# Moving the conditioning of batches 1 to 3 behind a transpose, and reordering a list of steps, in a gated quantised layer on one core

## The chip, the cores and the metric

The kernel runs on one core of a Trainium2 chip. A core has five engines with an instruction queue each: TensorE (PE, matmuls and transposes), VectorE (DVE), ScalarE (ACT), GpSimd (POOL) and SyncE (SP), which here only issues DMA transfers. Each queue is worked off strictly in its order, and the engines wait for one another on semaphores. The metric is the device time of one execution in microseconds (us), the median of several executions; lower is better.

## The reference

For `x` of 4 batches x 1024 tokens x 512, `cond` of 4 x 128, `norm_w` of 512 x 128, `up_w` of 4096 x 512 and `down_w` of 512 x 2048:

```python
scale = cond @ norm_w.T + 1.0                      # (batch, 512): the conditioning
ms = mean(x * x, axis=-1)
h = x * (scale[:, None, :] * rsqrt(ms + 1e-6))
val, gate = split(h @ up_w.T, 2)                   # 2048 each
h = val * gelu(gate)
hq = act_quant(h)                                  # 8 bit, one scale a token
wq = weight_quant(down_w)                          # -1, 0, 1 with one scale
y = hq @ wq.T + x
```

## The kernel before, in words

**Tiling.** The up projection is worked off in 16 slots a batch; a slot takes 128 columns of the gate and the 128 of the value that belong to them, against all 1024 tokens in two halves of 512. Operands are split in a high and a low float16 part, so that a product has twelve matmuls of 128x512 (two by four high-low terms and four high-high). In the first batch slots 0 to 13 are such plain products (`gate.j.h`, `value.j.h` for slot `j` and half `h`); later slots use a scheme with fewer products (`slot.g.n`), which needs sums of blocks of weights and of x that the first batch prepares. The down projection of a batch runs inside the slots of the next.

**Order of the work.** The order on every engine is written out by hand: instructions are issued in the order of the Python statements. Three pieces follow one another: the *head* (statements at the end of the function, from `first_load(0, 2)` on), `plain_first` (slot 0 for the first half of the tokens, with `second_part` and `second_slot` put between its matmuls), and `take(FIRST_BATCH)`, a string of 599 steps for slots 1 to 15 of the first batch. A step `name.a.b` calls an entry of the table `STEPS`; a name given to two engines has a last figure, 1 for VectorE and none for GpSimd. A step issues to whichever engines it needs, also to SyncE's queue.

**The head.** Loads go to SyncE: `norm_w`, x in four parts (`first_load`, two tiles of 128 tokens each), and the first weights (`w_load(0)` to `w_load(2)`). Meanwhile:

- `keep_warm(n)` runs `n` matmuls on zeros (`pz`, 128x512), whose result nobody reads.
- `cond_first_row` spreads `cond[0]` over the partitions by a matmul (`pc`), `cond_scale(0, pc)` multiplies and sums it with `norm_w` on VectorE, `cond_largest` takes the largest magnitude (`mx`), `cond_over` transposes that on TensorE (`pm`), `cond_range_steps` makes a power of two of it on VectorE, and `cond_spread` brings it to all partitions by a matmul (`pd`): the conditioning of batch 0.
- `cond_turn` transposes `cond` (`pc_t`) and `norm_w` in four blocks (`nw_t`) on TensorE and copies both out on ScalarE (`cT`, `nwT`). `cond_scale_rest` multiplies them in four small matmuls of float32 (`ps`, three columns each) and ScalarE adds 1 and writes `scT[:, :, 1:]`: the conditioning of batches 1 to 3. Its first reader is the step `c_largest` of the list.
- `first_sum` takes the sum of squares of a tile of x, `rsqrt_root` and `rsqrt_steps` its inverse root, `first_scale` scales the tile, `first_turn` transposes it on TensorE into the banks `ptx`, and `first_high` and `first_low` write its high and low parts with the conditioning (`XP`).
- `w_largest`, `w_factor_steps`, `w_scale`, `w_turn` (bank `pw`), `w_high` and `w_low` do the like with the weights of slot 0.

**The list.** `turn.n`, `x_scale.n`, `x_high.k` and `x_low.k` are the same for tiles 4 to 7. `w_load.j`, `w_range.j`, `w_factor.j` and `w_scale.j.t` load and scale the weights of slot `j`; `rows_high`, `rows_low` and `rows_turn` split them and transpose them by DMA; `s_sum.j.n`, `s_high.j.n`, `s_low.j.n` and `s_spill.j.n` make the sums of blocks and store them. `d_load.n` loads a part of `down_w` and `d_sum.n` sums its magnitudes on ScalarE; parts 2 and 3 go where `first_sum` writes its unread squares (`junk`). `o_*` and `t_*` prepare sums of x, `max.*` collects the largest magnitudes a token, `c_*` ends the conditioning of batches 1 to 3.

The lines of the profile that matter here: L1172 `keep_warm`, L207 `pc`, L185 and L189 `cond_turn`, L186 and L190 its copies, L197 and L202 `cond_scale_rest`, L228 `pm`, L253 `pd`, L1122 `first_sum` on ScalarE, L1149 `first_scale` on ScalarE, L1156 `first_turn`, L378 `w_turn`, L411 `w_high`, L1160 `first_high`, L779 the products of slot 0, L708 the plain products after it, L318 `w_range` on ScalarE, L302 `w_load` from 3 on, L305 the earlier ones, L511 `d_load`.

Of the kernel before, what the change touches and what calls it, by code (L numbers as in the profile page):

```python
# [14 lines left out]
AF = mybir.ActivationFunctionType  # L15
# [36 lines left out]
def glu_quant_kernel(  # L52
# [17 lines left out]
    NK = D // P  # L70
# [93 lines left out]
    def bank(tag, bufs, shape=None, name=None):  # L164
        return psum.tile(shape or [P, TOK], F32, name=name or tag, tag=tag, bufs=bufs)
# [26 lines left out]
    def cond_scale_rest():  # L192

        n = B - 1
        ps = bank("E", 2, name="ps")[:, : NK * n]
        for k in range(NK):
            PE.matmul(  # L197
                ps[:, k * n : (k + 1) * n], nwT[:, k * P : (k + 1) * P], cT[:, 1:B],
                start=True, stop=True,
            )  # L200
        v = ps.rearrange("p (k b) -> p k b", b=n)
        ACT.activation(scT[:, :, 1:], v, AF.Copy, bias=1.0)  # L202
# [145 lines left out]
    def w_range(j, t0=0, t1=2):  # L348
        w_factor(j, w_largest(j, t0, t1), t0, t1)
# [818 lines left out]
    def keep_warm(n):  # L1168

        pz = bank("A", 2, name="pz")  # L1170
        for i in range(n):
            PE.matmul(pz, warm[:, :P], warm, start=True, stop=True)  # L1172
# [10 lines left out]
    cond_turn()  # L1183
# [7 lines left out]
    cond_scale_rest()  # L1191
    keep_warm(4)
    steps = cond_range_steps(pm, 0, 1)
# [5 lines left out]
    keep_warm(7)  # L1199
# [69 lines left out]
    def next_turn(n):  # L1269
        if not made:  # L1270
# [75 lines left out]
    def take(steps):  # L1346
# [11 lines left out]
        o_WHOLE.3.2.1 w_range.4 d_load.0 rows_low.3 value.1.1 gelu.1.1 s_high.0.1 t_square.0.0 s_low.0.1.1  # L1358
        s_spill.0.0 s_sum.1.3.1 s_high.1.0 w_factor.4 w_load.10 w_range.5 out.0.1 rows_turn.3 gate.2.0
        s_low.1.0.1 s_high.1.1 w_scale.4.1 w_factor.5 s_low.1.1 out.1.1 d_sum.5 value.2.0 s_sum.2.1  # L1360
        w_scale.5.0 s_sum.2.0.1 w_scale.5.1 o_sum.0 d_sum.6 s_sum.2.2 c_over w_scale.4.0 gate.2.1 d_load.1
        c_range s_sum.2.3 s_spill.1.0 rows_high.4 s_spill.2.1 d_sum.7 w_gain.2 o_sum.1 gelu.2.0 value.2.1
        rows_low.4 o_high.1 out.2.0 w_gain.4 rows_high.5 o_low.1 w_load.6 gate.3.0 gelu.2.1 o_sum.2
        s_high.2.0 rows_turn.4 s_high.2.1 o_sum.3 o_high.2 value.3.0 o_high.3 rows_low.5 s_spill.3.1
        gelu.3.0 rows_turn.5 o_low.2 d_sum.2 gate.3.1 out.2.1 t_square.0.1 max.0.0.0 d_sum.3 t_root.0
        d_sum.0 s_low.2.0.1 s_spill.2.0 value.3.1 o_low.3 w_range.6 s_sum.3.0 w_load.7 d_sum.1 s_spill.4.1
        w_factor.6 s_low.2.1 w_load.11 w_scale.6.0 c_spread s_sum.3.1.1 s_spill.2.2 c_rows gate.4.0 out.3.0
        o_high.0 w_scale.6.1 o_low.0 gelu.3.1 rows_high.6 out.3.1 value.4.0 s_sum.3.2.1 w_range.7 max.1.0.0
        s_sum.3.3 w_load.8 s_high.3.1 rows_low.6 rows_turn.6 gelu.4.0 gate.4.1 s_high.3.0 s_low.3.0
        s_low.3.1.1 c_copy w_factor.7 w_scale.7.1 max.0.1.0 w_scale.7.0 t_load.1 value.4.1 out.4.0 s_sum.4.0  # L1370
        rows_high.7 rows_low.7 rows_turn.7 gelu.4.1 w_range.8 gate.5.0 s_sum.4.1.1 d_total s_sum.4.2.1
        out.4.1 s_high.4.0 s_sum.4.3.1 w_factor.8 s_spill.5.1 s_low.4.0 c_undo w_scale.8.1 c_store value.5.0
        s_sum.5.1.1 s_spill.3.2 w_scale.8.0 s_spill.6.1 w_gain.6 c_load gelu.5.0 s_sum.5.0.1 rows_high.8
        max.1.0.1 d_spread out.5.0 gate.5.1 w_range.9 rows_low.8 s_spill.7.1 s_high.4.1 s_low.4.1 max.1.1.0
        value.5.1 rows_turn.8 s_sum.5.2.1 s_high.5.0 s_sum.5.3.1 c_bring gelu.5.1 max.1.1.1 s_high.5.1
        s_low.5.0.1 gate.6.0 w_factor.9 s_sum.6.1 d_mean w_scale.9.0 t_scale.0.1 w_scale.9.1 out.5.1
        s_spill.5.0 t_high.0.1 s_spill.3.0 t_scale.0.0 value.6.0 gelu.6.0 s_spill.8.1 max.2.0.0 t_sum.0.1
        rows_high.9 s_low.5.1 t_high.0.0 s_sum.6.0.1 s_sum.6.2.1 s_high.6.0 gate.6.1 t_low.0.0 s_sum.6.3
        t_sum.0.0.1 rows_low.9 value.6.1 rows_turn.9 gelu.6.1 max.2.0.1 w_gain.8 t_sum.0.2.1 w_range.10
        t_sum.0.3 t_high.0.2 w_factor.10 gate.7.0 s_low.6.0.1 w_scale.10.1 out.6.0 w_scale.10.0 t_low.0.2  # L1380
        rows_high.10 s_spill.4.0 s_spill.5.2 value.7.0 t_low.0.1 t_turn.0 s_sum.7.1.1 out.6.1 rows_low.10
        w_range.11 gate.7.1 s_sum.7.0.1 s_sum.7.2 s_high.6.1 s_low.6.1.1 t_square.1.0 max.2.1.0 t_square.1.1
        s_sum.7.3 s_high.7.0 s_spill.4.2 t_root.1 value.7.1 s_spill.9.1 gelu.7.0 max.2.1.1 s_spill.6.0
        s_high.7.1 s_low.7.1 rows_turn.10 w_factor.11 s_low.7.0.1 gate.8.0 s_sum.8.0.1 s_sum.8.2.1 out.7.0
        gelu.8.0 max.3.0.0 s_spill.7.0 s_spill.6.2 value.8.0 s_sum.8.1.1 s_sum.8.3.1 w_gain.10 t_scale.1.1
        gelu.7.1 s_high.8.0 s_low.8.0.1 s_spill.8.0 s_high.8.1 gate.8.1 w_scale.11.1 w_scale.11.0
        s_sum.9.0.1 out.7.1 s_low.8.1.1 s_sum.9.2.1 value.8.1 s_sum.9.1.1 s_high.9.0 s_sum.9.3.1 w_load.12
        t_sum.1.0.1 s_low.9.0.1 rows_high.11 s_spill.8.2 w_range.12 rows_low.11 rows_turn.11 gate.9.0
        max.3.0.1 out.8.0 t_scale.1.0 value.9.0 s_spill.9.0 t_sum.1.1 gelu.8.1 t_load.2 gelu.9.0 w_factor.12
        s_spill.11.1 out.8.1 w_scale.12.1 s_sum.10.0.1 w_scale.12.0 t_sum.1.2.1 gate.9.1 s_high.9.1  # L1390
        s_sum.10.1.1 rows_high.12 t_sum.1.3 max.3.1.0 s_spill.7.2 s_low.9.1 t_high.1.2 s_sum.10.2.1
        max.3.1.1 t_high.1.1 value.9.1 s_high.10.0 s_sum.10.3.1 w_load.13 rows_low.12 t_high.1.0
        rows_turn.12 t_low.1.1 s_high.10.1 t_low.1.2 gelu.9.1 gate.10.0 w_range.13 t_low.1.0 out.9.0
        s_low.10.0.1 t_turn.1 value.10.0 max.4.0.0 s_sum.11.0 gelu.10.0 s_low.10.1 out.9.1 s_sum.11.2.1
        s_sum.11.1.1 s_high.11.0 max.4.0.1 gate.10.1 s_sum.11.3.1 t_square.2.1 s_low.11.0.1 s_sum.12.0
        s_spill.12.1 s_high.11.1 w_factor.13 w_load.14 s_spill.11.0 s_low.11.1.1 value.10.1 gelu.10.1
        s_sum.12.2.1 s_spill.10.1 t_load.3 t_square.2.0 w_scale.13.0 t_root.2 w_scale.13.1 s_sum.12.1
        gate.11.0 t_scale.2.1 out.10.0 t_high.2.1 s_spill.9.2 rows_high.13 t_scale.2.0 rows_low.13
        rows_turn.13 s_high.12.0 value.11.0 w_range.14 s_low.12.0.1 s_sum.13.1 t_high.2.0 out.10.1 gate.11.1
        w_factor.14 s_sum.12.3 w_scale.14.1 s_spill.10.2 t_low.2.1 s_sum.13.0.1 s_spill.10.0 w_scale.14.0  # L1400
        t_sum.2.1.1 s_spill.11.2 t_sum.2.0.1 w_gain.12 value.11.1 s_spill.12.0 s_sum.13.2.1 gelu.11.0
        t_sum.2.2 t_sum.2.3.1 w_load.15 gelu.11.1 s_high.12.1 out.11.0 s_high.13.0 s_low.13.0 s_spill.13.0
        out.11.1 gate.12.0 t_low.2.0 t_high.2.2 value.12.0 gelu.12.0 t_low.2.2 w_range.15 t_turn.2
        s_low.12.1 max.4.1.0 t_square.3.0 s_sum.14.1 gate.12.1 t_square.3.1 s_sum.13.3.1 w_factor.15
        rows_high.14 t_root.3 s_sum.14.0.1 max.4.1.1 s_sum.14.2 rows_low.14 value.12.1 gelu.12.1
        rows_turn.14 w_scale.15.1 w_scale.15.0 out.12.0 out.12.1 rows_high.15 gate.13.0 s_high.13.1
# [403 lines left out]
```

## Time and profile before

| | |
|---|---|
| median of 3 timed runs | 725.05 us (725.01, 725.05, 727.67) |
| the profiled execution's own time | 727.31 us |
| its span, first to last instruction | 725.4 us |
| TensorE busy | 718.4 us, 99% |
| VectorE, ScalarE, GpSimd busy | 584.5, 419.9, 139.1 us |
| DMA | 122.64 MB, mean 169 GB/s |

Of the views, the page gives busy times and shares; the waits say who stood still, for whom, in total, how often and the longest; the chain of waits follows the work that ended last back from the end; timelines give the start, the duration, engine, line and operation, output and inputs of instructions, and in brackets how long the engine stood idle before and what ended it. A matmul's duration includes its way through the array, so that consecutive matmuls overlap: the time that one costs is the distance between two starts.

### The profile page before, as it was taken

To read this page: it belongs to the slowest core of one execution; us is meant where nothing else is said; L and a number is where in the kernel's file an instruction comes from. 1 tells how busy PE (TensorE), PEld (TensorE's weight loads), DVE (VectorE), ACT (ScalarE), POOL (GpSimd) and SP (SyncE) were. 2 spreads that over 40 slices of the span, in tenths; PEclk is the share of its full clock that TensorE was granted. 3 is DMA by queue.
4 is the path that set the end of the run, shared out by engine and by line. 5 is a ranking of instruction groups with operands and counts; after the bars stand their busy time and mean duration, and the time that the engine had idled before them with its cause. 6 is when DMAs were issued, how large, how long until landed. Compare 5 with 4: busy or idle time off the path is not lost.

```text
span 725.4 us, 10231 instructions
## 1 busy us (share of the span) xinstructions
PE 718.4 (99%) x3679; PEld 362.7 (50%) x3679; DVE 584.5 (81%) x876; ACT 419.9 (58%) x697; POOL 139.1 (19%) x143
## 2 busy tenths in 40 slices
PE   8999999999999999999999999999999999999998
PEld 5444444444444446665444445666444444445854
DVE  6789799875898899788689887777678888765896
ACT  5899767774766775544335676544433665333463
POOL 1722231352100033540000030360020000000120
PEclk9999999999999999999999999999999999999999
DMA  7799978999995655877845647765955455453253
GB/s 275 261 246 275 249 184 242 277 204 259 290 200 122 131 122 152 198 182 153 189 101 103 131 101 175 203 148 155 218 97 112 103 102 102 102 100 99 102 166 126
DMA packets 228405, 122.64 MB, mean 169 GB/s; under 512 B 189801, under 2 KB 199805, under 8 KB 228354
## 3 DMA queue, kind: packets, MB, share of 16 engines
q1 hardware_dynamic: 228202, 121.85, 68.2%
q8 instruction: 29, 0.48, 0.3%
q14 instruction: 22, 0.18, 0.1%
q10 hardware_dynamic: 152, 0.13, 0.1%
HBM read 53.50 MB, written 23.09 MB: 106 GB/s over the span
## 4 chain that ended last, share of the span: by engine, by line
PE 93%; DVE 4%; ACT 1%; DMA 1%; issue 0%; SPq 0%
PE A L693 33%; PE E L693 17%; PE pv L708 9%; PE po L1055 9%; PE pg L708 9%; PE B L693 9%; PE po_end L1007 4%; DVE gm L899 1%; PE pz L1172 1%; DMA H<-in_L_cond_up_w_dram 1%; DVE R L901 1%; DVE R L894 1%; ACT R L1160 1%; DVE H L828 0%; DVE t L836 0%
## 5 line engine op out<-in xcount | busy, mean ns | idle before, releaser
L693 PEld LDWEIGHTS <-SXY 128*128 128x128 f16 x2058 | 201.4, 98 | 236.0 <-issue 0.7
L693 PE MATMUL A<-R,SXY 128*128 128x512 f16 x1158 | 267.4, 379 | 0.0
L693 PE MATMUL E<-R,SXY 128*128 128x512 f16 x582 | 141.4, 379 | 0.1
L828 DVE SCALAR_TENSOR_TENSOR H<-A,sg,t 128x512 f32<-128x512 f32 x50 | 37.5, 749 | 72.0 <-PE A L693 71.8
L979 DVE TENSOR_TENSOR H<-H,am 128x1024 f32<-128x1024 f32 x64 | 76.1, 1214 | 0.0
L839 ACT ACTIVATE t<-t,sg 128x512 f32<-128x512 f32 x50 | 36.1, 721 | 65.9 <-DVE t L836 65.8
L693 PE MATMUL B<-R,SXY 128*128 128x512 f16 x294 | 71.5, 379 | 0.0
L899 DVE TENSOR_REDUCE gm<-H 128x512 f32<-128x1024 f32 x56 | 69.0, 1233 | 0.9
L708 PEld LDWEIGHTS <-SXY 128*128 128x128 f16 x438 | 42.8, 98 | 53.3 <-issue 1.9
L915 POOL PARTITION_ALL_REDUCE am<-R x8 | 14.4, 1795 | 229.3 <-DVE R L901 229.3
L822 ACT ACTIVATE t<-B,sg 128x512 f32<-128x512 f32 x50 | 34.4, 687 | 38.8 <-PE B L693 38.2
L708 PE MATMUL pg<-R,SXY 128*128 128x512 f16 x228 | 52.7, 379 | 1.3 <-ACT R L1160 1.3
L1055 PE MATMUL po<-wd,R 128*128 128x256 fp8e4 x416 | 52.4, 273 | 0.0
L708 PE MATMUL pv<-R,SXY 128*128 128x512 f16 x210 | 48.9, 379 | 0.0
L815 ACT COPY t<-A 128x512 f32<-128x512 f32 x50 | 29.0, 581 | 34.3 <-PE A L693 33.9
L1055 PEld LDWEIGHTS <-R 128*128 128x128 bf16 (+1 forms) x448 | 43.8, 98 | 8.9
L808 ACT COPY v<-E 128x512 f32<-128x512 f32 x50 | 29.3, 586 | 32.0 <-PE E L693 28.4
L800 ACT COPY B<-A 128x512 f32<-128x512 f32 x50 | 28.6, 572 | 31.7 <-PE A L693 31.1
L848 DVE SCALAR_TENSOR_TENSOR H<-v,sg,t 128x512 f32<-128x512 f32 x50 | 39.3, 786 | 7.2 <-ACT t L839 7.2
L845 DVE TENSOR_TENSOR v<-A,v 128x512 f32<-128x512 f32 x50 | 34.1, 683 | 13.1 <-PE A L693 11.9
L987 ACT ACTIVATE H<-H 128x1024 f32<-128x1024 f32 x38 | 39.9, 1050 | 5.2 <-DVE H L979 5.2
L901 DVE TENSOR_TENSOR R<-R,gm 128x512 f32<-128x512 f32 x56 | 40.7, 727 | 1.0
(237 smaller groups left out, 935.3 us busy)
## 6 DMA issues: line engine op xcount, KB each, us to landing
SXY<-s_dram SPq DMA_DIRECT2D x48, 256.0 KB, 3.0
H<-in_L_cond_up_w_dram SPq DMA_DIRECT2D x13, 512.0 KB, 5.5
s_dram<-SXY SPq DMA_DIRECT2D x17, 384.0 KB, 3.4
SXY<-s_dram SPq DMA_DIRECT2D x48, 128.0 KB, 3.4
xr<-in_x_dram SPq DMA_DIRECT2D x19, 256.0 KB, 3.2
out_dram<-xr SPq DMA_DIRECT2D x19, 256.0 KB, 3.0
H<-in_x_dram SPq DMA_DIRECT2D x8, 512.0 KB, 5.3
R<-in_L_cond_down_w_dram SPq DMA_DIRECT2D x8, 512.0 KB, 7.4
```

Of the source, the lines that this page charges most:

```text
L693: PE.matmul(o, s[:, w, k, :], operand(g // NJ, c, l, k), start=start and n == 0, stop=stop and n == len(TERMS) - 1, skip_group_check=True,)
L708: PE.matmul(ps, a[k // 2][:, w, k % 2, :], XP[:, l, k, h * TOK : (h + 1) * TOK], start=n == 0, stop=n == len(terms) - 1,)
L822: ACT.activation(self.t1, self.B, AF.Gelu, scale=gain(self.g, 1))
L828: DVE.scalar_tensor_tensor(h_half(self.g, 0), self.A, gain(self.g, 0), self.t1, ALU.mult, ALU.mult)
L839: ACT.activation(self.t2, self.t2, AF.Gelu, scale=gain(self.g, 1))
L845: DVE.tensor_tensor(self.v, self.A, self.v, ALU.add)
L848: DVE.scalar_tensor_tensor(h_half(self.g, 1), self.v, gain(self.g, 0), self.t2, ALU.mult, ALU.mult)
L899: DVE.tensor_reduce(gm[0], v, AX.X, ALU.max, apply_absolute_value=True)
L901: return [largest, lambda: DVE.tensor_tensor(m, m, gm[0], ALU.max)]
L979: DVE.tensor_tensor(v, v, r.to_broadcast([P, 2, TOK]), ALU.mult)
L987: ACT.activation(v, v, AF.Copy, bias=MAGIC)
L1055: PE.matmul(po, w[:, j], m, start=start and j == 0, stop=stop and j == n - 1, skip_group_check=True,)
```

## The change

In the head, `cond_turn` moves from ahead of the second group of idle matmuls to behind the fourth call, that is behind `cond_over` (the transpose of the maximum). The matmuls of `cond_scale_rest` are taken apart: those for blocks 0 and 1 go between idle matmuls behind `cond_spread`, where instead of seven idle matmuls there are two groups of two; those for blocks 2 and 3 go behind the transpose of slot 0's gate weights, and the ScalarE operation that ends them behind `w_high(0, (1,))`. There are 16 idle matmuls for 19. A test in `next_turn` is written differently and does the same.

```diff
-    def cond_scale_rest():
+    def cond_scale_rest(ps, ks):
         n = B - 1
-        ps = bank("E", 2, name="ps")[:, : NK * n]
-        for k in range(NK):
+        for k in ks:
             PE.matmul(
                 ps[:, k * n : (k + 1) * n], nwT[:, k * P : (k + 1) * P], cT[:, 1:B],
                 start=True, stop=True,
             )
-        v = ps.rearrange("p (k b) -> p k b", b=n)
-        ACT.activation(scT[:, :, 1:], v, AF.Copy, bias=1.0)
...
-    def keep_warm(n):
-        pz = bank("A", 2, name="pz")
+    def keep_warm(n, pz=None):
+        pz = pz or bank("A", 2, name="pz")
...
     pc = cond_first_row()
-    cond_turn()
     keep_warm(5)
     cond_scale(0, pc)
...
     root = rsqrt_root(0, 2)
-    cond_scale_rest()
     keep_warm(4)
+    cond_turn()
     steps = cond_range_steps(pm, 0, 1)
...
     pd = cond_spread(dg, 0, 1, "A")
-    keep_warm(7)
+    ps = bank("E", 2, name="ps")[:, : NK * (B - 1)]
+    pz = bank("A", 2, name="pz")
+    for k in range(2):
+        cond_scale_rest(ps, (k,))
+        keep_warm(2, pz)
     first_sum(2)
...
     w_turn(0, [bank("E", 2, name=f"pw_0_{t}") for t in (1, 0)], (1,))
+    cond_scale_rest(ps, (2, 3))
     w_range(0, 0, 1)
     first_high(0, 0, ptx[0])
     w_high(0, (1,))
+    ACT.activation(
+        scT[:, :, 1:], ps.rearrange("p (k b) -> p k b", b=B - 1), AF.Copy, bias=1.0
+    )
     w_scale(0, (0,))
```

The list has the same 599 steps in another order. Most steps move by a few places. Eight change their engine: `s_sum.0.3`, `s_sum.1.0`, `s_sum.14.2` and `s_sum.15.2` go from GpSimd to VectorE, `s_sum.1.3`, `s_sum.8.1`, `s_low.8.1` and `s_low.15.0` from VectorE to GpSimd. Its beginning, up to the second slot:

```diff
-        d_load.6 d_load.5 d_load.3 w_load.3 d_load.4 t_load.0 d_load.7 s_sum.0.0 o_whole.2.2.0 gate.1.0
-        x_scale.6 w_range.3 x_scale.7 s_sum.0.1 gelu.1.0 turn.4 turn.5 w_load.4 w_factor.3 s_sum.0.2 turn.6
-        w_range.2 turn.7 o_whole.0.0.0 w_load.5 x_high.0 value.1.0 x_high.3 x_low.0 d_load.2 x_high.1
-        s_high.0.0 w_factor.2 s_sum.0.3 w_load.9 x_high.2 s_low.0.0 x_low.1 w_scale.2.1 x_low.2 w_scale.2.0
-        x_low.3 gate.0.1 o_whole.1.0.1 w_scale.3.1 out.1.0 rows_high.2 value.0.1 gelu.0.1 rows_low.2
-        rows_turn.2 d_sum.4 s_sum.1.0 w_scale.3.0 gate.1.1 s_sum.1.1.1 rows_high.3 s_sum.1.2 c_largest
+        d_load.7 w_load.3 d_load.3 d_load.5 d_load.4 t_load.0 d_load.6 s_sum.0.0 o_whole.2.2.0 gate.1.0
+        x_scale.6 w_range.3 x_scale.7 s_sum.0.2 turn.4 w_range.2 turn.5 w_load.4 s_sum.0.1 turn.6 w_factor.3
+        turn.7 o_whole.0.0.0 d_load.2 x_high.0 value.1.0 w_load.5 gelu.1.0 x_low.0 x_high.1 x_high.2
+        w_factor.2 x_low.1 x_high.3 w_scale.2.1 x_low.3 o_whole.1.0.1 s_high.0.0 x_low.2 gate.0.1
+        w_scale.2.0 out.1.0 w_scale.3.1 s_low.0.0 value.0.1 rows_high.2 w_scale.3.0 rows_low.2 rows_turn.2
+        rows_high.3 s_sum.1.0.1 gate.1.1 w_range.4 o_WHOLE.3.2.1 s_sum.1.1.1 d_sum.4 s_sum.0.3.1 d_load.0
+        rows_low.3 w_load.9 gelu.1.1 value.1.1 s_sum.1.2 c_largest t_square.0.0 gelu.0.1 s_high.0.1
```

More of the change, by code (lines that the diff above doesn't have):

```diff
@@ L1357, in glu_quant_kernel @@
-        rows_turn.2 d_sum.4 s_sum.1.0 w_scale.3.0 gate.1.1 s_sum.1.1.1 rows_high.3 s_sum.1.2 c_largest
[L1358 to L1371, printed above, removed]
@@ L1387, in glu_quant_kernel @@
[L1387 to L1396, printed above, removed]
@@ L1402, in glu_quant_kernel @@
[L1402 to L1406, printed above, removed]
@@ new lines, in glu_quant_kernel @@
+        rows_turn.3 w_scale.4.1 w_factor.5 s_high.1.1 out.1.1 value.2.0 d_sum.5 s_low.1.1 w_scale.5.1
+        s_low.1.0.1 d_sum.6 s_sum.2.1 w_scale.4.0 c_over s_sum.2.0.1 s_sum.2.2 gate.2.1 o_sum.0 w_gain.4
+        d_sum.7 c_range s_spill.1.0 rows_high.4 s_sum.2.3 d_load.1 s_spill.2.1 value.2.1 w_scale.5.0
+        w_gain.2 o_sum.1 gelu.2.0 out.2.0 o_high.1 rows_low.4 rows_turn.4 gelu.2.1 gate.3.0 rows_high.5
+        o_low.1 s_high.2.0 o_sum.2 s_high.2.1 value.3.0 o_sum.3 o_high.2 w_load.6 o_high.3 rows_low.5
@@ new lines, in glu_quant_kernel @@
+        rows_turn.5 gelu.3.0 gate.3.1 out.2.1 d_sum.2 o_low.3 d_sum.3 max.0.0.0 s_spill.3.1 t_square.0.1
+        value.3.1 d_sum.0 o_low.2 w_range.6 t_root.0 s_low.2.0.1 s_spill.2.0 c_spread d_sum.1 c_rows
+        gate.4.0 w_load.7 w_factor.6 s_sum.3.0 s_spill.4.1 w_scale.6.0 out.3.0 w_load.11 o_high.0 s_low.2.1
+        s_spill.2.2 s_sum.3.1.1 w_scale.6.1 o_low.0 value.4.0 gelu.3.1 rows_high.6 out.3.1 s_sum.3.2.1
+        s_sum.3.3 w_range.7 max.1.0.0 gate.4.1 w_load.8 s_high.3.1 rows_low.6 rows_turn.6 gelu.4.0
@@ new lines, in glu_quant_kernel @@
+        s_spill.10.1 s_sum.11.2.1 s_sum.11.1.1 s_high.11.0 gate.10.1 max.4.0.1 s_sum.11.3.1 t_square.2.1
+        s_low.11.0.1 s_sum.12.0 s_spill.12.1 s_high.11.1 w_load.14 gelu.10.1 w_factor.13 s_spill.11.0
+        s_low.11.1.1 value.10.1 s_spill.9.2 s_sum.12.2.1 t_load.3 t_square.2.0 w_scale.13.0 t_root.2
+        t_scale.2.1 w_scale.13.1 s_sum.12.1 gate.11.0 t_high.2.1 out.10.0 rows_high.13 t_scale.2.0
+        rows_low.13 rows_turn.13 s_high.12.0 value.11.0 w_range.14 s_low.12.0.1 s_sum.13.1 t_high.2.0
```

79 lines of the change are left out of this document (46 added, 33 removed).

## The prediction

> **What bounds the kernel now.** I read the page first, then TensorE's waits, then the chain of waits in order of time, then the timelines of the first 34 us by engine. The page:
>
> ```profile
> span 725.4 us, 10231 instructions
> PE 718.4 (99%) x3679; PEld 362.7 (50%) x3679; DVE 584.5 (81%) x876; ACT 419.9 (58%) x697; POOL 139.1 (19%) x143
> PEclk9999999999999999999999999999999999999999
> ```
>
> TensorE (PE) is busy in all but 7 us. Everything it waits for in the whole span stands in one view, its waits (total us, times, longest):
>
> ```profile
> PE pz L1172 <- DVE eps L1102: 1.5, 1, 1.5
> PE pg L708 <- ACT R L1160: 1.3, 2, 0.9
> PE pg L779 <- ACT SXY L411: 0.7, 1, 0.7
> PE pg L779 <- ACT R L1160: 0.2, 1, 0.2
> ```
>
> So a change of order can gain in two places: these waits, all in the first 33 us, and time in which PE is busy with idle matmuls (`pz`) or runs slowly. After that PE never waits for another engine, and a reordering there can only lose. The chain of waits through the head (start, us, what):
>
> ```profile
> 3.72 0.01 PE pc_t L185
> 3.73 1.04 PE nw_t L189 x4
> 4.77 2.13 PE pz L1172 x5
> 6.91 0.21 PE pm L228
> 7.12 1.50 PE ps L197 x8
> 8.62 1.73 PE pz L1172 x4
> 10.35 0.51 PE pd L253 x2
> 10.86 2.46 PE pz L1172 x7
> 13.32 1.75 PE ptx L1156 x16
> 15.07 0.45 PE pw L378 x4
> ```
>
> Two readings. First, idle matmuls stand directly ahead of the transposes of x (`ptx`), though x was ready: ScalarE ends its three scalings at 11.61 (9.68 + 1.93, below), and `ptx` begins at 13.32. PE's own queue sets the head. Second, PE doubles its pace on the way: a 128x128 transpose takes 0.26 us in `nw_t` (1.04/4) and 0.11 in `ptx` (1.75/16); `pz` goes from 0.43 (1.73/4) to about 0.22. The granted clock on the page reads full throughout, so only the spacing shows it. Three looks at PE's timeline, each row beginning at the first matmul then running:
>
> ```profile
> 12.05 0.85 PE L1172 MATMUL pz<-H 128*128 128x512 f16 x2
> 12.47 0.85 PE L1172 MATMUL pz<-H 128*128 128x512 f16 x3
> 12.73 0.59 PE L1172 MATMUL pz<-H 128*128 128x512 f16 x2
> ```
>
> Starts at 12.05, 12.47, 12.73: the pace doubles near 12.5, some 4 us into the idle matmuls that began at 8.62 (only `pd` between). The nine earlier ones were split by `nw_t` and `ps` and did not do it.
>
> **The head, part by part.** The timelines of ScalarE (ACT) and VectorE (DVE), and the first product on PE:
>
> ```profile
> 4.81 0.59 ACT L190 COPY R<-nw_t 128x512 f32<-128x512 f32 x1 [0.85 <-PE nw_t L189]
> 8.66 0.18 ACT L202 ACTIVATE scT<-ps 128x12 f32<-128x12 f32 x1 [1.65 <-PE ps L197]
> 8.73 0.62 ACT L1122 ACTIVATE R<-H 128x512 f32<-128x512 f32 x1
> 9.68 1.93 ACT L1149 ACTIVATE H<-H,rs 128x512 f32<-128x512 f32 x3
> 5.29 0.16 DVE L221 TENSOR_REDUCE mx<-scT 128x1 f32<-128x4 f32 x1
> 7.16 0.28 DVE L236 TENSOR_REDUCE d<-pm 1x1 f32<-1x128 f32 x1 [0.55 <-PE pm L228]
> 16.19 0.39 PE L779 MATMUL pg<-R,SXY 128*128 128x512 f16 x1 [0.68 <-ACT SXY L411]
> ```
>
> *`cond_turn` moved behind `pm`.* 1.05 us of PE (0.01 + 1.04) leaves the place ahead of the five `pz`; they now end at 5.85, and `pm` runs to 6.06 since `mx` is ready at 5.45. DVE loses its wait of 0.55. The four `pz` end at 7.79 and `pc_t`, `nw_t` at 8.84 at the slow pace. What is new: ACT's copy of `nwT` (0.59) ends at 9.46, and behind it in ACT's queue stands the sum of squares that ran at 8.73, so ACT's chain slips by 0.73 and its scalings end at 12.34. `pd` (0.51) fits beside the copy.
>
> *`cond_scale_rest` split, `pz` 19 to 16.* PE now waits for the copy (9.46), then two steps of 0.38 (a quarter of 1.50) and four `pz` of 0.43: 0.76 + 1.73, so `ptx` begins at 11.96, 1.36 us earlier. The first scaling is there at 9.68 + 0.73 + 0.64 = 11.05. The two later steps lie behind `pw` in PE's wait of 0.7 for ACT and cost nothing; uncovered they would be 0.75. ACT's `scT` (0.18, of which 0.07 shows: 8.66 to 8.73) now stands ahead of three casts that PE needs: +0.1. Its reader, `c_largest`, stands in the list behind `gate.1.1`, far from it.
>
> What that gives depends on when the pace doubles, which no trace shows for the new order. Bounds from the rows:
> - as late as now (12.5): 0.54 us of `ptx` at 0.21, then 13.5 at 0.11 = 1.47, `pw` 0.45: end 14.42 for 15.52. Head -1.1 + 0.1 = -1.0.
> - inside the nine `pz` that now stand almost together from 3.72 to 7.79 (4.07 us with 0.21 of `pm`, as long as the stretch that did it before): `pc_t` and `nw_t` take 0.5, the copy ends at 8.92, ACT slips by 0.19 only; `ptx` is then paced by the scalings, the last at 11.80, and ends at 12.24 for 15.07: -2.8 + 0.1 = -2.7.
>
> I take -2.4: the nine stand as dense as the run that worked, and 0.3 is kept back because `pw` still waits for GpSimd's scaling of the weights and the loads arrive when they did.
>
> The Trainium skill, "TensorE: Matmul & The Clock Gate", Part 1, says the same of the mechanism: the array runs at half rate until one free-running window of about 3.4 us has been busy. The trace agrees: the pace doubled after 3.9 us of unbroken idle matmuls. Taken strictly the rule speaks against the value above, since 4.07 us contain a whole window of 3.4 only in one phase of five (0.67 of 3.4), and the head would then give -1.0 in the others; by the row, where `pd` did not spoil the stretch, it gives -2.4.
>
> **The list.** The same 599 steps. SyncE's queue in the head, what it waited for, the median time of such a load to landing, and the stretch on ACT and PE that follows:
>
> ```profile
> 8.26 12.45 SPq L511 DMA_DIRECT2D R<-in_L_cond_down_w_dram  x3
> 20.76 0.43 SPq L302 DMA_DIRECT2D H<-in_L_cond_up_w_dram  x1
> SPq L511 <- ACT R L1122: 10.2, 1, 10.2
> R<-in_L_cond_down_w_dram SPq DMA_DIRECT2D x7, 512.0 KB, 7.7
> 27.34 0.63 ACT L318 ACTIVATE H<-H 128x512 f16<-128x512 f32 x1 [2.64 <-DMA H<-in_L_cond_up_w_dram]
> 26.82 1.04 PE L1156 MATMUL ptx<-ident,H 128*128 128x128 f32 x8
> 30.29 0.38 PE L708 MATMUL pg<-R,SXY 128*128 128x512 f16 x1
> 31.04 0.38 PE L708 MATMUL pg<-R,SXY 128*128 128x512 f16 x1 [0.37 <-ACT R L1160]
> 32.35 1.89 PE L708 MATMUL pg<-R,SXY 128*128 128x512 f16 x8 [0.94 <-ACT R L1160]
> ```
>
> Of the three issues from 8.26 the third, `d_load.3`, writes where the sums of squares put their junk, and waits 10.2 us for the last. `w_load.3` stood behind it, issued at 20.76; ACT waited 2.64 for it at 27.34, with four casts of x behind that, and PE lost 0.37 + 0.94 = 1.31. Now `w_load.3` is second, ahead of `d_load.3`. It takes the place of a load of the same size issued within a microsecond of 8.26, so it is there near 17 (7.7 from issue to landing), against a need at 24.7 (27.34 less 2.64). ACT's wait of 2.64 goes; next late for the casts is PE's own transpose of x (26.82 + 1.04 = 27.9), and four casts with one GELU, at about the scalings' 0.64, end at 31.1, when PE asks for the last one (30.29 + three of 0.22 = 30.95). I take -1.3; the ends are -1.31 and 0. `d_load.6`, `d_load.5` go the other way, into the burst that `d_load.3` opens near 20; they are first read by `d_sum`, behind `gate.1.1`. `d_load.2` passes `w_load.5`, which lands one load of 512 KB later for it; its reader `w_range.5` stands several products behind.
>
> Behind that the list has reorderings within a slot and eight changes of engine, four each way, between GpSimd and VectorE:
>
> ```profile
> L432 DVE TENSOR_TENSOR H<-H x37: 405/417/949, 36.5 to 158.9; 128x256 f32<-128x256 f32 x37
> L432 POOL TENSOR_TENSOR H<-H x27: 723/730/3647, 22.5 to 165.3; 128x256 f32<-128x256 f32 x27
> 33.00:60.00 27.00, 27.00 (x127) 12.29 (x126) 24.06 (x37) 26.63 (x50) 9.56 (x10) 1.00 0.92 257
> 90.00:120.00 30.00, 30.00 (x141) 13.59 (x139) 28.39 (x50) 20.26 (x41) 7.24 (x10) 1.00 0.80 211
> ```
>
> (The last two: stretch, then busy time of PE, PEld, DVE, ACT, POOL.) At 0.42 against 0.73 us each the exchange evens out, and neither engine is ever waited for by PE. ACT from 33 to 60 (26.63 of 27) and DVE from 90 to 120 (28.39 of 30) are the covers that could fail. The first comes in 2.64 us better off. Bounds 0 and +1.3, the wait that PE knew here when a load was late; I take 0.
>
> **Sum.** Against the profiled execution's own 727.31 us: -2.4 - 1.3 + 0 = 723.6; with the bounds -4.0 to +0.3. That execution lies 2.26 above the median of the timed runs (725.05) and near their highest (727.67). I read the lower runs as ones without the late load or with an earlier doubling, that is with part of the gain already in them, and so keep 723.7 and not 725.05 - 3.7.
>
> **Rivals.**
> - *The doubling comes too late (slower).* The idle matmuls behind `nw_t` come in twos now, between small steps and a wait; if the nine do not do it, nothing dense follows until the products. `ptx` and `pw` then take 20 x 0.21 = 4.2 from 11.96, the first product follows 0.68 later, near 16.9 for 16.19 (+0.8 with `scT`), and every further us at the slow pace costs half. With 1.3 won at the load it decides from 18.0 on; at 22.7 it is +0.8 + 2.85 - 1.3 = +2.3: 729.6. For it: the earlier nine `pz` failed when split. Against: unsplit, they are as long as the run that worked. The same page of the Trainium skill (Part 4) holds that transposes do not count as activity, which this trace allows (`nw_t`, slow, brought nothing) and which speaks for this rival.
> - *Doubling where it was.* -1.0 - 1.3: 725.0.
> - *The gain adds to the median.* If the 2.26 are the profile's own cost, 725.05 - 3.7 = 721.4. Against it: a timed run reached 727.67 without one.
> - *A new wait in the list.* One cast or turn late in slots 1 to 3 takes the 1.3 back: 725 to 726.5. PE's waits show no margin to judge it by, only that there was none.
>
> **How the numbers follow.** Forecast 723.7 with 0.45, the later doubling 0.17, the gain on the median 0.13, too late 0.15, a new wait 0.10. A measurement here tells about 0.5% (3.6 us) from no change: under 721.4 is half of the third case and some of the first, 0.14; over 728.7 is most of the too-late case and a little of the last, 0.14; between, 0.72. The range 721.0 to 728.3 takes in all but the ends of both; the likeliest case alone has 722.5 to 725.
>
> **What would show it.** Right: `ptx` begins at 10.5 to 12, L776 (the old L779) before 15.3, `w_load.3` issued near 9, no wait of PE on ACT near 31, and none later. The spacing of the second group of `pz` tells the clock: 0.43 to the end, with transposes of 0.21, is the too-late case. A wait of PE between 33 and 180 us is the new wait. Wrong altogether: spans of PE's work that differ after 180 us, where nothing was edited.

## The result, and the profile after

The changed kernel takes 723.91 us (median of 20 timed executions, 722.68 to 726.55), the kernel before 725.37 (20 executions in turn with them, 724.56 to 729.50): a ratio of 0.9973, 95% interval 0.9961 to 0.9985. The profiled execution of the changed kernel took 724.24 us with a span of 722.5, against 727.31 and 725.4 before.

First the page of the changed kernel (span; busy time of the engines) and the waits of PE (for whom; us in total, times, longest):

```profile
span 722.5 us, 10223 instructions
PE 716.2 (99%) x3676; PEld 360.7 (50%) x3676; DVE 584.4 (81%) x876; ACT 420.0 (58%) x697; POOL 139.4 (19%) x143
```

```profile
PE pz L1169 <- DVE eps L1099: 1.5, 1, 1.5
PE ps L196 <- ACT R L190: 0.4, 1, 0.4
PE pg L776 <- ACT SXY L408: 0.3, 1, 0.3
PE pg L776 <- ACT R L1157: 0.3, 1, 0.3
PE A L690 <- DMA SXY<-s_rows: 0.2, 1, 0.2
PE ptx L1153 <- ACT H L1146: 0.2, 1, 0.2
```

The line numbers of the old code fall by 3 (L779 is now L776, L708 is L705, L1172 is L1169). PE's wait of 1.31 us in L708 is gone. New are a wait of PE for the copy of `nwT` (L190), one for the first scaled tile (L1146), and one of 0.2 for sums of blocks read back from device memory, at 178 us.

The chain that ended last, in the head (start, us, what):

```profile
6.19 1.66 PE pz L1169 x4
7.84 0.15 PE pc_t L185
7.99 0.60 PE nw_t L189 x4
...
8.62 0.59 ACT R L190
9.20 0.33 ACT R L1119
...
10.15 0.62 ACT H L1146
...
10.82 2.14 PE ptx L1153 x16
12.96 0.45 PE pw L375 x4
```

PE no longer holds the chain all the way from 3 to 15 us: ScalarE does from 8.62 to 10.82, with the copy of `nwT`, a sum of squares, a root and a scaling. The four `nw_t` take 0.60 where they took 1.04, and the sixteen `ptx` and four `pw` start 0.11 apart, but for one wait for the second scaled tile at 11.4.

The timeline after, the rows that answer to those of the prediction (start, us, engine, line, operation; in brackets the idle time before it):

```profile
14.07 0.39 PE L776 MATMUL pg<-R,SXY 128*128 128x512 f16 x1 [0.34 <-ACT SXY L408]
28.18 2.75 PE L705 MATMUL pg<-R,SXY 128*128 128x512 f16 x12
```

```profile
9.42 0.38 SPq L299 DMA_DIRECT2D H<-in_L_cond_up_w_dram  x1
```

```profile
22.54 0.64 ACT L315 ACTIVATE H<-H 128x512 f16<-128x512 f32 x1
```

The first product begins at 14.07 for 16.19: -2.12. `w_load.3` is issued at 9.42 for 20.76, ScalarE's `w_range.3` finds its data at once, and the twelve matmuls that were broken by idle times of 0.37 and 0.94 run as one. That is worth more than the 1.31 of idle time, since what a matmul costs is the distance between two starts: the starts at 30.29, 31.04 and 32.35 lie 0.75 and 1.31 apart where the full pace has 0.216, so the late load cost 1.63. With equal products compared, the two executions are 3.73 apart at 35 us.

Of this the changed kernel gives back 0.74: late starts of 0.07, 0.15 and 0.10 at 85.99, 101.68 and 104.38, too short to show as idle time (no row says what they waited for), and 0.40 at 178 us, where two groups start 1.69 apart that take 1.30 elsewhere:

```profile
176.90 1.46 PE L690 MATMUL E<-R 128*128 128x512 f16 x6
178.59 1.47 PE L690 MATMUL A<-wd,SXY 128*128 128x512 f16 x6 [0.24 <-DMA SXY<-s_rows]
```

From 183 us to the end the two executions are apart by a constant 3.0.

### The profile page after: what moved, and what is told of

Same layout as the page of the kernel before. It is cut to its first block, busy times and chain, and to the rows that moved or that the text cites. A ratio compares the mean times of both kernels' runs of the same rounds, so it can differ in the third digit from the quotient of the medians.

```text
span 722.5 us, 10223 instructions
## 1 busy us (share of the span) xinstructions
PE 716.2 (99%) x3676; PEld 360.7 (50%) x3676; DVE 584.4 (81%) x876; ACT 420.0 (58%) x697; POOL 139.4 (19%) x143
## 4 chain that ended last, share of the span: by engine, by line
PE 96%; DVE 2%; DMA 1%; ACT 1%; SPq 0%; issue 0%
PE A L690 34%; PE E L690 17%; PE pg L705 10%; PE pv L705 10%; PE po L1052 9%; PE B L690 9%; PE po_end L1004 4%; DMA SXY<-s_rows 1%; PE pz L1169 1%; DVE gm L896 1%; PE ptx L1153 1%; PE pv L776 0%; PE po_B L1052 0%; DVE R L898 0%; PE pg L776 0%; DVE R L891 0%
## 5 line engine op out<-in xcount | busy, mean ns | idle before, releaser
L705 PEld LDWEIGHTS <-SXY 128*128 128x128 f16 x438 | 42.8, 98 | 51.6 <-DVE SXY L417 0.4
L705 PE MATMUL pg<-R,SXY 128*128 128x512 f16 x228 | 52.4, 379 | 0.0
L705 PE MATMUL pv<-R,SXY 128*128 128x512 f16 x210 | 48.9, 379 | 0.0
```

The source lines that it names most:

```text
L705: PE.matmul(ps, a[k // 2][:, w, k % 2, :], XP[:, l, k, h * TOK : (h + 1) * TOK], start=n == 0, stop=n == len(terms) - 1,)
```

## The experiments

Each timed set ran in turn with the kernel before on the same chip. Two numbers are read from each profile: when the first product of slot 0 begins (L779 or L776), and when TensorE's pace doubles, that is when matmuls of 512 columns go from 0.43 us apart to 0.22, and small ones and transposes from 0.21 to 0.11. The rows below merge equal matmuls; the moment of doubling is read from the starts of the single ones in the trace, and from the granted clock that the trace keeps with them.

**The head alone.** The changed kernel with the old list:

```diff
     FIRST_BATCH = """
-        d_load.7 w_load.3 d_load.3 d_load.5 d_load.4 t_load.0 d_load.6 ...
+        d_load.6 d_load.5 d_load.3 w_load.3 d_load.4 t_load.0 d_load.7 ...
```

> The new head with the list of the kernel before. Theory A (two gains that add: the head by the earlier doubling of PE's pace, the load by its place in SP's queue): the profile shows the doubling between 7 and 8.5 us and the first product (L776) between 13.5 and 14.6 as in the changed kernel (14.07), while w_load.3 is again issued behind the wait of SP for the last sum of squares (past 18 us) and PE loses 0.8 to 1.5 us to late casts near 30. Time: about 0.9 us under the kernel before at the median, 2.1 under it in a profile like the one shown. Rival B (the head's gain is eaten by the load: everything behind waits for the load, whatever the head does): the first product is early, but PE's waits near 30 grow by the 2.1 us won, and the time equals the kernel before within 0.5 us. Rival C (the list's other reorderings hold a part of the gain): more than half of the gain is missing here and in the run that moves the load alone.

Measured: 724.86 us (724.35 to 725.53), ratio 0.9965 (0.9953 to 0.9977), span 723.4. Timeline of PE, SyncE's queue and ScalarE:

```profile
13.83 0.39 PE L776 MATMUL pg<-R,SXY 128*128 128x512 f16 x1 [0.34 <-ACT SXY L408]
...
28.74 1.24 PE L705 MATMUL pg<-R,SXY 128*128 128x512 f16 x5 [0.22 <-ACT R L1157]
30.95 1.69 PE L705 MATMUL pg<-R,SXY 128*128 128x512 f16 x5 [0.96 <-DVE R L1161]
```

```profile
18.47 0.43 SPq L299 DMA_DIRECT2D H<-in_L_cond_up_w_dram  x1
```

```profile
23.74 0.63 ACT L315 ACTIVATE H<-H 128x512 f16<-128x512 f32 x1 [1.32 <-DMA H<-in_L_cond_up_w_dram]
```

The head's gain is there (13.83) and the wait for the load stays: 0.22 + 0.96 on PE. By the distances between starts it costs 1.97 for 1.63 in the kernel before. So it grows by 0.3 and not by the 2.4 that the head won, because the load is issued behind the last sum of squares, which comes earlier too (18.47 for 20.76). Rival B falls. The ten times lie within 1.2 us of each other, where those of the kernel before spread over 5.2 (724.31 to 729.49 in this set).

**The list alone.** The kernel before with the new list:

```diff
     FIRST_BATCH = """
-        d_load.6 d_load.5 d_load.3 w_load.3 d_load.4 t_load.0 d_load.7 ...
+        d_load.7 w_load.3 d_load.3 d_load.5 d_load.4 t_load.0 d_load.6 ...
```

> The old head with the new list. Theory A: the head as before (doubling near 12.5 us, first product 15.8 to 16.4), w_load.3 issued near 9 and no wait of PE on ACT near 31; 1.3 us less than the kernel before in a profile like the one shown, 0.3 to 1.3 less at the median, the less the more of the timed runs have no late load anyway. Rival B: the list alone takes nearly all of what the changed kernel gained, 1.2 us or more at the median. Rival C cannot be told from A here, only beside the next run.

**One step of it.** The kernel before with `w_load.3` second and nothing else moved:

```diff
     FIRST_BATCH = """
-        d_load.6 d_load.5 d_load.3 w_load.3 d_load.4 ...
+        d_load.6 w_load.3 d_load.5 d_load.3 d_load.4 ...
```

> The kernel before with one step moved: w_load.3 second in the list, ahead of d_load.3, all else as it was. Theory A: the same as with the whole new list within 0.4 us, w_load.3 issued near 9, no wait of PE near 31. Rival C (the other reorderings matter): the wait near 31 is gone, but the time differs from that of the whole new list by more than 0.5 us, either way; the new list also has a wait of PE of 0.24 for a copy from device memory near 178 us, which should be missing here and be worth at most 0.24.

Measured: the list 725.71 us (722.92 to 727.10), ratio 0.9975 (0.9959 to 0.9991); the one step 724.44 (722.82 to 725.78), ratio 0.9971 (0.9955 to 0.9987). PE's timeline of the list alone:

```profile
8.49 1.87 PE L1172 MATMUL pz<-H 128*128 128x512 f16 x4
...
15.93 0.39 PE L779 MATMUL pg<-R,SXY 128*128 128x512 f16 x1 [0.68 <-ACT SXY L411]
...
30.03 2.75 PE L708 MATMUL pg<-R,SXY 128*128 128x512 f16 x12
```

and of the one step, whose span is 721.5 where the list's is 724.2:

```profile
4.15 0.64 PE L189 MATMUL nw_t<-ident,R 128*128 128x128 f32 x2
4.57 2.34 PE L1172 MATMUL pz<-H 128*128 128x512 f16 x5
6.71 0.42 PE L228 MATMUL pm<-ident,mx 128*1 128x128 f32 x1
6.92 1.25 PE L197 MATMUL ps<-R 128*128 128x3 f32 x8
8.03 1.02 PE L1172 MATMUL pz<-H 128*128 128x512 f16 x4
...
13.84 0.39 PE L779 MATMUL pg<-R,SXY 128*128 128x512 f16 x1 [0.68 <-ACT SXY L411]
```

Both lose the wait near 31 (the twelve at 30.03 run as one). But the head is *the same old head* in both, and in the second the pace doubled at 7.5 us, in the midst of `ps`, instead of at 12.0: four `pz` take 1.02 for 1.87, and the first product comes at 13.84, as early as with the new head. The timed executions say the same. The one step gives six at 722.8 to 723.5 and six at 725.4 to 725.8; the list four at 722.9 to 723.8 and eight at 725.6 to 727.1; nothing in between. So the old head doubles early in some executions and late in others, about 2.4 us apart, and what the new head brings is not what the prediction said of it, a fixed gain. Rival C (other reorderings) can be read only between executions that agree in the head; that comes below.

**The kernel before again,** unchanged.

> The kernel before, unchanged, as one more kernel. Its ratio shows what such a comparison tells from nothing: 1.000 within 0.001. Its profile shows what varies from execution to execution: by theory A the doubling of the pace near 12.5 and the landing of w_load.3, and an execution without the late load has a span up to 1.3 us under the 725.4 shown. If the profile repeats both waits and the span of 725.4, then the lower timed runs are not explained by the load, and profiled executions are simply longer than timed ones.

Measured: 725.92 (724.51 to 728.36), ratio 0.9994 (0.9978 to 1.001), span 725.1: doubling at 12.0, first product at 15.95, and PE stood idle for 0.23 + 0.93 at late casts. The comparison tells 0.2% from nothing. Its own lower times (724.5 to 725.1) lie some 1.6 above those of the run with the load moved, its upper ones spread to 728.4.

From here the theory was another one (L): the pace is a lottery by execution. Four kernels tested it. **The changed kernel again:**

> The changed kernel once more. Theory L (a lottery that the new head mostly wins: PE's pace doubles at the end of a stretch whose place differs from execution to execution, if that stretch was filled with idle matmuls of 512 columns): most executions between 722.7 and 724.8, at most one in four near 725.5 to 726.5, none between. Rival S (the order of work alone sets when the pace doubles, and the spread of the kernel before comes from loads that land late): no second group at all, the times spread about evenly over 2 us.

Measured: 723.70 us (723.00 to 724.68, six executions), ratio 0.9953 (0.9937 to 0.9969); the kernel before stood at 727.19 in this set.

```profile
6.02 1.39 PE L1169 MATMUL pz<-H 128*128 128x512 f16 x4
...
13.68 0.39 PE L776 MATMUL pg<-R,SXY 128*128 128x512 f16 x1 [0.34 <-ACT SXY L408]
```

The doubling came at 6.8, inside the second group of idle matmuls; at 7.7 in the profile shown first, hence 13.68 for 14.07. The wait at 178 us is absent. Its span, 721.6, equals that of the one-step kernel (721.5), which has the old list but for the load: between two executions with an early head, the first product comes 0.16 earlier here and the last one 0.02 later. So *all other reorderings of the list cost 0.2 us* in this pair, and they do not cost the same in every execution. From 35 us on, the one-step kernel, the exchange below and the new head with the old list lose nothing to the kernel before; of the profiles with the new list, late starts take 0.7 in the one shown first, 0.7 with the list alone, 0.2 here, and in kernels below 0.2 with `cond_turn` moved back, 0.6 with transposes and none with the matmuls of three columns. Rival C is right that the rest of the list matters, and it is a loss: nothing to 0.7 us. Of all 26 timed executions of the changed kernel 23 lie at 722.7 to 724.8 and three at 725.5 to 726.6. Rival S (one spread, no groups) is out by the two groups of the one-step kernel.

**Four idle matmuls ahead of `ps`.** The one-step kernel with two lines exchanged:

```diff
-    cond_scale_rest()
     keep_warm(4)
+    cond_scale_rest()
```

> The kernel with the load alone moved, and in it the four idle matmuls ahead of the eight small matmuls (ps) instead of behind them; the same instructions. The run with the load alone fell into two groups, 722.8 to 723.5 and 725.4 to 725.8. Theory L: nine idle matmuls then stand together from 4.6 to 8.6 us, broken only by pm, and every place of the stretch catches enough of them: the upper group is gone (at most one execution in ten), all between 722.8 and 724.3, the pace doubles between 6.5 and 9 us. ACT's sum waits for ps, which costs up to 0.4. Rival N (any work of PE counts, small matmuls too): the swap changes nothing, two groups in the old proportion. Rival S: one group, but 725 or later, since the work is the same.

Measured: 723.52 us (723.13 to 724.27, six executions), ratio 0.9949 (0.9935 to 0.9963), span 721.5.

```profile
6.71 0.38 PE L228 MATMUL pm<-ident,mx 128*1 128x128 f32 x1
6.97 1.02 PE L1172 MATMUL pz<-H 128*128 128x512 f16 x4
...
13.85 0.39 PE L779 MATMUL pg<-R,SXY 128*128 128x512 f16 x1 [0.68 <-ACT SXY L411]
```

The upper group, half of the times without the exchange, is absent in these six: same instructions, nine idle matmuls together, broken only by `pm`. This one exchange does what the changed head does.

**Without the four.** The changed kernel with five idle matmuls in a row only:

```diff
     root = rsqrt_root(0, 2)
-    keep_warm(4)
     cond_turn()
```

> The changed kernel without the four idle matmuls between pm and cond_turn. Left in a row are the five from 3.7 to 5.8 us, 2.1 us, as long as the five of the kernel before that were followed by small matmuls. Theory L: two groups again, about half each; the early one at 723 to 724 (the copy of nwT comes a microsecond earlier, but VectorE's chain holds the scalings), and the late one worse than before, since nothing dense follows until the products: transposes at 0.21 and first products at 0.43, 726 to 728. Rival N or S: the early group alone, 723 to 724, since pm, the transposes and the small matmuls keep PE busy as well.

Measured: 724.17 us (722.43 to 728.76), ratio 0.9966 (0.9949 to 0.9983); the profiled execution was the slowest of the twelve, span 727.0. Its timeline, and a table by stretches (stretch; its length and the busy time of PE, PEld, DVE, ACT, POOL, each with its instructions; granted clock; DMA share; GB/s):

```profile
9.98 0.70 PE L1169 MATMUL pz<-H 128*128 128x512 f16 x2
10.86 3.35 PE L1153 MATMUL ptx<-ident,H 128*128 128x128 f32 x16 [0.18 <-ACT H L1146]
```

```profile
7.00:10.35 3.35, 1.70 (x12) 1.05 (x10) 3.02 (x15) 2.62 (x9) 0.00 (x0) 1.00 1.02 370
10.35:13.75 3.40, 3.22 (x16) 2.89 (x15) 3.19 (x18) 1.69 (x3) 0.96 (x2) 0.50 1.06 409
13.75:17.00 3.25, 2.65 (x18) 1.79 (x17) 2.13 (x5) 3.00 (x7) 0.99 (x1) 1.00 0.70 274
```

```profile
89.18 2.75 PE L705 MATMUL pg<-R,SXY 128*128 128x512 f16 x12 [1.84 <-DVE wmean L525]
```

The pace doubled at 6.9 us, *fell back* near 10.35 and doubled again near 13.75: three moments 3.4 us apart, with 0.50 granted in the whole stretch between the last two and 1.00 on both sides. Ahead of the fall lies a stretch in which PE was busy for 1.70 of 3.35; the stretch that brought the pace back held almost nothing but transposes of x.

The trace keeps the granted clock as intervals, of which the views print the mean, and these show where the lottery is drawn. In this execution the full clock lasts 3.413 us and then the half clock 3.413. In all fourteen profiles the interval of full clock that runs to the end of the kernel lasts 709.97, 713.39 or 716.80 us, which is 208, 209 or 210 times 3.413. So in these profiles the clock changes only on a grid of 3.413 us, and the grid lies elsewhere in each execution: its first change comes at 12.04, 12.46, 12.54 and 15.12 in four executions of the kernel before, at 6.79 and 7.66 in two of the changed one. That the work between two lines of the grid decides whether the pace doubles at the second fits all fourteen, if the one-row matmuls `pc` are left out of that work; no run could set the grid.

The first product came at 15.32. A second loss lies far from the head: VectorE delivered `wmean` 1.84 too late at 89 us, a wait that no other profile here has; what delayed VectorE was not traced. The expectation's two groups did not come out: of the twelve times, 722.4 to 728.8, one is above 726, where half were expected. But the mean granted clock of each execution tells two kinds apart. Six of the twelve have 0.998, which is what one stretch of 3.413 us at half clock takes off, and no execution of another kernel has less than 0.999. The median of these six is 724.64, that of the other six 723.53.

**`cond_turn` in its old place,** with all else of the changed kernel:

```diff
     pc = cond_first_row()
+    cond_turn()
     keep_warm(5)
...
     keep_warm(4)
-    cond_turn()
```

> The changed kernel with cond_turn back in its old place ahead of the five idle matmuls; ps stays split and behind. Nine idle matmuls stand together from 4.6 to 8.6 us, and ACT's copy of nwT is done by 5.5 and off its chain. Theory L: one group at 722.7 to 723.7, without the executions at 725.5 to 726.5 that the changed kernel still has; median 0.3 to 0.8 us under the changed kernel's. If the copy on ACT's chain was of no weight, the lower edge stays at 722.7. Rival S or N: the doubling depends on cond_turn's place (1.05 us of transposes early): near 12 us, 725 to 726.

Measured: 723.66 us (722.91 to 724.37, six executions), ratio 0.9949 (0.9935 to 0.9964), span 721.6; doubling at 6.6.

```profile
10.41 2.15 PE L1153 MATMUL ptx<-ident,H 128*128 128x128 f32 x16 [0.78 <-ACT H L1146]
```

```profile
8.65 0.63 ACT L1119 ACTIVATE R<-H 128x512 f32<-128x512 f32 x1 [1.62 <-DMA H<-in_x_dram]
```

Moving `cond_turn` was not what helped: with it back the group is as tight and the first product as early (13.67). The 0.3 to 0.8 us expected under the changed kernel's median did not come: ScalarE gains nothing by being rid of the copy, since it then waits 1.62 for the second part of x. None of the three (the changed kernel, the exchange, this one) is measurably ahead of the others.

Last, what counts towards the doubling. Nine idle matmuls of the changed kernel **replaced by eighteen transposes,** and by **eighteen matmuls of three columns,** whose bank nobody reads either:

```diff
+    def keep_busy(n):
+        pz = bank("A", 2, name="pz")
+        for i in range(2 * n):
+            PE.transpose(pz[:, :P], ident, ident)
+            # second kernel instead:
+            # PE.matmul(pz[:, :3], ident, ident[:, :3], start=True, stop=True)
...
-    keep_warm(5)
+    keep_busy(5)
...
-    keep_warm(4)
+    keep_busy(4)
```

> The changed kernel with the nine idle matmuls from 3.7 to 7.8 us replaced by eighteen f32 transposes of a 128x128 tile, two for one, which take as long (0.21 each at the slow pace, as nw_t). Theory W (the pace is set anew every 3.4 us or so by what the stretch behind held, and transposes of 128 columns count like idle matmuls; small matmuls of 3 columns do not): the pace doubles between 6.3 and 9.7 us as with the idle matmuls, the first product at 13.5 to 14.5 us, all executions between 722.7 and 724.8. Rival K (transposes do not count, the first line of thought in the prediction's too-late case): ptx runs at 0.21 each, the first product comes after 15.5 us, 725.5 to 729.

> The same with eighteen f32 matmuls of 3 columns in the nine's place, the size of ps, which take 0.21 each as well, so that PE's queue is as full as before. Theory W: they do not bring the doubling; it comes at the earliest when the transposes of x fill a stretch, past 12 us; first product after 15 us, 725 to 729 in nearly all executions. Rival N (any work that keeps PE's queue busy counts): as the changed kernel, 722.7 to 724.8.

Measured: transposes 724.38 us (eleven of twelve at 723.1 to 724.9, one at 726.99), ratio 0.9971 (0.9955 to 0.9987); three columns 730.11 (729.64 to 731.12), ratio 1.0054 (1.0034 to 1.0074). The timelines, transposes first:

```profile
6.11 1.97 PE L1169 MATMUL pz<-ident 128*128 128x128 f32 x8
...
11.40 2.14 PE L1153 MATMUL ptx<-ident,H 128*128 128x128 f32 x16 [0.15 <-ACT H L1146]
```

```profile
3.65 4.43 PE L1169 MATMUL pz<-ident 128*128 128x3 f32 x20
...
8.14 3.58 PE L1169 MATMUL pz<-ident 128*128 128x3 f32 x16
...
15.98 3.62 PE L1153 MATMUL ptx<-ident,H 128*128 128x128 f32 x16
...
21.10 0.39 PE L776 MATMUL pg<-R,SXY 128*128 128x512 f16 x1 [0.34 <-ACT SXY L408]
```

With transposes alone from 3.65 on (and `pm`) the pace doubled at 8.9, and the first product came at 14.66 (expected by 14.5). The small matmuls were mis-sized: a float32 one of three columns is two records of 0.21, so the block was twice as long as meant, and the 730 us hold some 4 us of that length. The answer is the clearer for it: PE's queue was never empty from 3.65 to 12.5, and the pace did not double before 20.2, behind twenty transposes. Rivals K (transposes do not count) and N (anything counts) fall.

**The kernel before twice more, one profile each.**

> The kernel before once more, one look, to see a profile of its lower group of times if this execution belongs to it. Theory W: either a span of 722.5 to 723.5 with the doubling between 6.5 and 8.2 us and the late load still there, or one of 724.5 to 726.5 with the doubling between 11.5 and 13 us; nothing else. Rival S: the span varies with the load while the doubling stays near 12.

> As the third look at the kernel before, for the same question: an early doubling with a span of 722.5 to 723.5, or a late one with 724.5 to 726.5 (theory W), or a doubling always near 12 (rival S).

Measured: 727.84 us (span 726.1) and 729.47 (span 727.6). PE's timeline of the second:

```profile
8.48 1.87 PE L1172 MATMUL pz<-H 128*128 128x512 f16 x4
10.28 0.58 PE L253 MATMUL pd<-dg,one 1*128 1x1 f32 x2
10.80 3.17 PE L1172 MATMUL pz<-H 128*128 128x512 f16 x7
13.76 2.58 PE L1156 MATMUL ptx<-ident,H 128*128 128x128 f32 x16
...
17.45 0.39 PE L779 MATMUL pg<-R,SXY 128*128 128x512 f16 x1 [0.68 <-ACT SXY L411]
```

The first doubled at 12.5, the second only at 15.1, in the midst of `ptx`: all seven idle matmuls at the slow pace. Neither expected span holds the second, so theory W's "nothing else" was too narrow, though the cause is its own: doubling late, a first product 1.3 us later, and PE standing idle for 1.8 at the late load. An early execution of the kernel before itself was not caught in a profile (four late ones); its early head was seen in the one-step kernel, whose head is the same code.

## Why the prediction was right, step by step

The forecast was 723.7; measured 723.91 (and 723.70 in the second set). The two causes that it named are there, an earlier doubling and an earlier load. That the number came so near is in part luck. In the profiled pair the head gave -2.1 for -2.4 and the load -1.6 for -1.3, which cancel, and the rest of the list gave +0.7 for 0: together -3.0 for -3.7. In the repeat the same three are -2.5, -1.6 and +0.2, together -3.9. And the sum starts from a profile that happened to be a late execution.

- *What bounds it.* As told. PE's queue of idle matmuls set the head in a late execution, and the late load cost PE idle time in every profile that has it behind `d_load.3`: 1.31, 1.16, 1.4 and 1.8 in the kernel before, 1.18 with the new head.
- *The head, -2.4.* Measured -2.12 in the profiled pair and -2.51 in the repeat. Of the two bounds it was the one "inside the nine `pz`", as taken. The times ahead of the doubling held: the four `pz` ended at 7.84 (7.79). Missed were 0.28 at the copy of `nwT` (ended 9.20, not 8.92): `pc_t` and `nw_t` took 0.15 + 0.60 and not 0.5, though they ran at the full pace. Another 0.44 was missed at `ptx`, which ended at 12.96 and not at 12.24 + 0.28: behind the second scaling twelve of the sixteen still stood in a row, where the prediction had four left behind the last one. The 0.3 kept back for `pw` and the loads covered part of this by luck, since `pw` followed `ptx` without a wait. ScalarE's `scT` showed as 0.08, taken as 0.1.
- *What kind of gain it is.* This step failed. The prediction took the doubling as a property of the order of work: before at 12.5, after at 7 to 8, with rivals for other places. In fact the old order itself wins or loses by execution (7.5 to 15.1 in six profiles with that head), and the new order makes the win likely, 23 of 26. So -2.4 is what an execution gains that would have been late, and nothing one that would not. The medians of the kernel before, 725.37, 726.88, 727.19 and 727.11 in the four sets, move with the share of late executions. The sentence that the lower timed runs hold part of the gain already was right, and by it 723.7 was kept and 721.4 refused. Of its two reasons the earlier doubling was the one; no profile of the kernel before lacked the late load.
- *The list.* `w_load.3` was issued at 9.42 (near 9) and landed 7.7 later (near 17), and the wait is gone in all nine profiles with the load moved, early or late: this is the sure part of the gain. But -1.3, with -1.31 as the far end, was mis-sized, because it adds up idle times; by the distances between starts the late load cost 1.63, 1.49, 2.19 and 2.52 in the kernel before. The rest of the list, taken as 0, cost nothing to 0.7, and 0.7 in the profiled pair; the prediction itself had said that a reordering behind 33 us can only lose. VectorE from 90 to 120 was named as a cover that could fail; near it, at 89 us, it did in one kernel, for 1.84.
- *The rivals.* "Too late" did not happen in the changed kernel's profiles, and its mechanism is real: 17.45 for the first product in the latest profile of the kernel before. Its argument by transposes was wrong, they count. "Doubling where it was" and "the gain adds to the median" fell by 23 of 26 executions between 722.7 and 724.8. "A new wait in the list" was there, in size 0.7 at most and not 1.3.
- *The Trainium skill.* The Trainium skill, "TensorE: Matmul & The Clock Gate", Part 1, has a free-running window of about 3.4 us. The trace agrees, with 3.413 us at a granted clock of 0.50 between two changes and a grid that lies elsewhere in each execution. The prediction's strict reading (a whole window busy, one phase in five) does not hold. Between two lines of the grid, the kernel before had 2.8 of 3.41 us in idle matmuls ahead of 12.54, with `pd` among them, and doubled; the one-step kernel had 2.8 of idle matmuls, transposes and `pm` ahead of 7.54 (from the rows: `nw_t` to 4.57, five `pz` to 6.71, `pm` 0.21) and doubled; the last profile had about 2.7 ahead of 11.70 and did not. By these the bar lies near 80%, an estimate. It leaves out the small matmuls and `pc`, whose operand is a single row: with the 0.4 of `pc` the stretch from 2.30 to 5.71 of the kernel before would hold 2.9, and it did not bring the doubling. That `pc` does not count was not tested. The Trainium skill, same page, Part 4, says that transposes do not count as busy; here the doubling at 8.9 us and the stretch at 0.50, which held almost nothing but transposes and brought the pace back, say otherwise, and the measurement decides.

Open: the exact bar and what a matmul weighs by its columns; and the three executions of the changed kernel at 725.5 to 726.6, of which no profile was caught (nine idle matmuls in two groups leave a place for the stretch to end late, up to about 9.7, is the argument, not a finding).

## What to carry to other kernels

A span that comes in two groups a fixed distance apart points to a lottery, and one profile of each kernel cannot tell a change in its odds from a change in the work: take the times of many executions first, and compare profiles of the same outcome. At the start of a kernel, put the idle matmuls in one dense row with small matmuls behind, not between (here nine of them, 4 us, with transposes ahead, left no late execution in six of each of two kernels). In a queue that issues in order, look for the load that stands behind a waiting one and is needed sooner; it was 1.5 to 2.5 us in every profile, for one step moved. And read the cost of a wait from the distance between starts: the idle time showed 1.31 where 1.63 was lost, and nothing where 0.1 was.

## What the runs showed of the hardware

TensorE's pace can fall back in the head of a kernel after a stretch of 3.35 us with PE busy for 1.70 of it; its longest single pause there was 1.65. A float32 matmul of three columns, two records of 0.21, keeps the queue full and does not bring the pace up in 8 us; transposes of 128x128 do. In all fourteen profiles the clock changed only on a grid of 3.413 us, whose place differs from execution to execution. The granted clock of the profile read 1.00 through the slow beginning of every execution, though matmuls ran at half the pace: its record begins only with the first doubling (12.54 us in the kernel before), and only after that did it show the fall (0.50). The pace of the matmuls, not that column, tells the clock at the start of a kernel.
